# Experts' last biases gathered per slot, and rows gathered by a table of token ids, in a two-layer attention and mixture-of-experts kernel

## The chip, the cores and the metric

The kernel runs on one core of a Trainium2 chip. The metric is the device time of one execution in microseconds (us). Engines are called as in the profile: PE is the matmul engine and PEld its weight load, DVE the vector engine, ACT the scalar engine, POOL the GpSimd engine; SP issues most DMA transfers. POOL issues the indirect ones, whose rows are chosen by a list of indices in on-chip memory. On-chip memory has 128 partitions; sums of matmuls are made in PSUM banks[...].

## The reference

All arrays are fp32. There are 8 sequences of 256 tokens, 2048 tokens of 512 channels. Layer 0 adds a linear attention with decay and a mixture of experts to its input; layer 1 adds a small attention and a low-rank feed-forward part with gates. What the change touches is the mixture of experts of layer 0, cut to what matters:

```python
scores = softmax(xt @ router_w + router_b) + router_bias
g = scores.reshape(T, 4, 4)                   # 16 experts in 4 groups
keep the 2 groups with the largest maximum; of them the 2 best experts per token
gate[token, expert] = scores where chosen, else 0
for w1, b1, w2, b2, w3, b3, ge in experts:    # 512 -> 128 -> 512
    h = silu(xt @ w1 + b1) * (xt @ w2 + b2)
    y = y + ge[:, None] * (h @ w3 + b3)
z = silu(xt @ sw1 + sb1) * (xt @ sw2 + sb2) @ sw3 + sb3   # shared expert, all tokens
x = x + attention(xn) + y + z
```

The third biases are thus 16 rows b3 of 512 numbers, each added with the token's gate, and one row sb3 that every token gets once. The kernel's input `b3` holds them as 17 rows, the shared one last.

## The kernel before, in words

**Tiling.** Tokens are handled in 4 chunks of 512 (NCH = 4, `i` counts them), each of 4 tiles of 128 tokens (TPC = 4, `t` counts them; 16 tiles in all, NTT).

**The opening (to about 200 us).** The loop over chunks at lines 423–442 does, per chunk: transposes of the normalized rows on PE (`turn_rows`, L243), the store of the rows to DRAM (`xnd`), token differences on POOL (`token_sums`), the shared expert's first matmuls (`shared_up`, projected at L312), and `route` (matmuls at L271, then a chain on DVE: scores, `first_two` over groups, `first_two` over experts, the gates `ge`). Then `decays(i)`, `clear(i)`, and `share(i - 1)` for the chunk before. `share` calls `shared_down`, L329–341: it turns the gates with a column of ones (17 columns) by four transposes L333, ACT copies them to `geT` (L335), and for every tile a matmul L338 multiplies the turned gates with the 17 rows of b3 (two PE instructions each) ahead of the shared expert's own last matmul L340 into the same bank. So y's bias term and sb3 enter x here. DVE adds the bank to x, and x goes to DRAM as `xr`. `clear(i)` writes zeros over a fourth of `xd`, a DRAM array of 6016 slots of 512 numbers, 47 tiles of 128 slots.

**The dispatch.** Lines 447–523, mostly on DVE, give each token's two choices a slot so that every tile of 128 slots belongs to one expert: `slots` (token to slots), `slot_gates` (the two gates), `rows_` (which rows of the packed expert weights a tile needs). `before`, a table for ties, `sel_all` (the choices) and the gates live in the pool `work1` of the opening, which is given back by `opening.close()` at L525; the attention part's pool gets the same memory, so its first writes there wait for the dispatch.

**The long part (to about 2560 us).** A plan of units (chunk, group of heads) with seven products each (p1 to p7; Strassen's scheme, `product`, L666) runs inside a schedule in which ACT and POOL keep the written order, and PE, DVE and SP are ordered by a scheduler. `slot()`, L679, is called after each product: a slot takes about 1.39 us, 49 of them make a unit. In each slot up to one or two pieces of other work are written in, from a list to which `later(after, f)` adds `f`, due `after` slots on; pieces named in a tuple in `slot` don't count against that limit. Chunk 0 is computed with plain products while the weights' sums for the later chunks are made. In it, `row` loads each tile of normalized rows from `xnd` and `scatter` (L1094) writes it twice, by `slots`, into `xd` with indirect DMAs.

From the eighth unit on (chunk 1), `expert(j)` is written in for each of the 47 tiles, three per unit in seven units, two per unit after that. `Expert.__init__` takes a staging buffer `xw` (two exist, shared with other staging), loads the tile's rows from `xd` by SP (L696) and gathers the expert's weights by POOL (L697); `turn` (+8 slots) transposes the rows on PE (L706), `up` (+11) makes 8 matmuls (L716), silu on ACT, the product `he` on DVE; `down` (+14) multiplies by the third weight (L728), ACT copies the bank to `ye` (L733), SP stores it to `yd`.

At a chunk's end, `load_sum` (L933) loads `xr` into a staging buffer, and `done` (L939) makes the norm's root mean squares and `finish` (L586) adds the attention's sum to it on DVE; the result is stored as `xs_`. For the last chunk `next_x(3)` (L1289) loads `xr` and finishes it inside layer 1. `gather` and `settle` later fetch from `yd` each token's two rows and add them with `slot_gates`.

Of the kernel before, what the change touches and what calls it, by code (L numbers as in the profile page):

```python
# [66 lines left out]
def block_kernel(  # L67
# [75 lines left out]
    def once(shape, name):  # L143
        return work.tile(shape, FP, tag=name, name=name, bufs=1)

    scratch = big("scratch").rearrange("p (h b) n -> p h (b n)", h=4)
# [18 lines left out]
    b3_t = held[0 : E + 1, SH * C : (SH + 1) * C]  # L165
    nc.sync.dma_start(out=b3_t, in_=b3)
# [8 lines left out]
    xd = dram.tile([NSLOT, C], FP, name="xd")  # L175
# [7 lines left out]
    xnd = [dram.tile([P, TPC, C], FP, name=f"xnd{i}") for i in range(NCH)]  # L183
# [5 lines left out]
    zero = held[:, (SH + 1) * C : (SH + 2) * C].unsqueeze(1)  # L189
    nc.gpsimd.memset(zero, 0.0)  # L190
# [10 lines left out]
    before = once([P, E, E], "before")  # L201
# [8 lines left out]
    dist = const.tile([P, S + P], FP, name="dist")  # L210
# [54 lines left out]
    def route(xT, ge, sel):  # L265
# [40 lines left out]
        tt(ge[:, :, 0:E], sc, sel, ALU.mult)  # L306
        nc.vector.memset(ge[:, :, E : E + 1], 1.0)
# [21 lines left out]
    def shared_down(i, hT):  # L329
        xc = xs[i]  # L330
        pg = ps_sc()
        for t in range(TPC):
            nc.tensor.transpose(pg[0 : E + 1, bass.ts(t, P)], gates[i][:, t, :], ident)  # L333
        gT = work.tile([E + 1, CH], FP, tag="geT", name="geT", bufs=1)
        nc.scalar.copy(gT, pg[0 : E + 1, :])  # L335
        for t in range(TPC):
            py = ps_mm()
            mm(py, gT[:, bass.ts(t, P)], b3_t, start=True, stop=False)  # L338
            for e in range(SH):
                mm(py, hT[:, e, bass.ts(t, P)], w3sh[:, e, :], start=False, stop=(e == SH - 1))  # L340
            tt(xc[:, t, :], py, xc[:, t, :], ALU.add)
# [3 lines left out]
    sel_all = once([P, NTT, E], "sel_all")  # L345

    def share(i, hT):
        shared_down(i, hT)
        nc.sync.dma_start(out=xr[i], in_=xs[i])
# [60 lines left out]
    def clear(i):  # L410
        lo, hi = (0, 12, 24, 36, NMT)[i : i + 2]
        nc.sync.dma_start(
            out=xd[lo * P : hi * P, :].rearrange("(j p) c -> p j c", p=P),
            in_=zero.to_broadcast([P, hi - lo, C]),
        )

# [6 lines left out]
    for i in range(NCH):  # L423
        xT.append(work.tile([P, NC, CH], FP, tag="xT", name=f"xT{i}", bufs=3))
        for t in range(TPC):
            turn_rows(xT[i], xns[i], t, ps_mm())
        nc.sync.dma_start(out=xnd[i], in_=xns[i])
        if i + 1 < NCH:
            begin(i + 1)
        token_sums(i)  # L430
        if i == 0:
            for p in ORDER[0:2]:
                w = big("w")
                nc.sync.dma_start(out=w[:, 0:4], in_=w_att[0, RAW[p]])
                first_w.append(w)
        ups.append(shared_up(i))
        ge = once([P, TPC, E + 1], f"ge{i}")
        route(xT[i], ge, sel_all[:, bass.ts(i, TPC), :])
        gates.append(ge)
        decays(i)  # L440
        clear(i)
        if i > 0:
            share(i - 1, ups[i - 1])
# [6 lines left out]
    disp = Parts(accp.tile([P, 7 * CH], FP, tag="acc", name="disp"))  # L450
# [50 lines left out]
    nc.vector.tensor_reduce(own, owner, AX.X, ALU.add)  # L501
    nc.vector.tensor_scalar(own, own, float(E - 1), float(P), ALU.min, ALU.mult)
# [14 lines left out]
    for n in range(TOP):  # L517
        tt(hit, slot, ends_[:, n, :].unsqueeze(2).to_broadcast(full), ALU.is_equal)
        tt(hit, hit, sel_all, ALU.mult)
        for i in range(NCH):  # L520
            at_i = bass.ts(i, TPC)
            tt(hit[:, at_i, :], hit[:, at_i, :], gates[i][:, :, 0:E], ALU.mult)
# [63 lines left out]
    def finish(i, r):  # L586

        for b in range(2):
            for t in range(2):
# [4 lines left out]
                )  # L594

# [3 lines left out]
    with tc.tile_pool(name="attn", bufs=1) as attn, tc.manual_schedule(engines={mybir.EngineType.Activation, mybir.EngineType.Pool}):  # L599
# [79 lines left out]
        def slot():  # L679
# [3 lines left out]
            while pieces and pieces[0][0] <= now[0] and n < (2 if len(pieces) > 12 else 1):  # L683
                f = pieces.pop(0)[2]
                f()
                n += getattr(f, "func", f).__name__ not in ("silu", "gate", "row", "scatter", "load_sum", "sums1", "sums2", "sums3", "sums4", "settle0", "settle1", "out_sum")


        class Expert:


            def __init__(self, j):
# [3 lines left out]
                nc.sync.dma_start(out=self.xe, in_=xd[bass.ts(j, P), :])  # L696
# [6 lines left out]
            def turn(self):  # L703
# [4 lines left out]
                nc.vector.tensor_copy(self.xeT, pt.rearrange("p (c n) -> p c n", c=NC))  # L708

# [16 lines left out]
            def down(self):  # L726
# [6 lines left out]
                nc.scalar.copy(ye, py)  # L733
# [76 lines left out]
        class Unit:  # L810
# [122 lines left out]
            def load_sum(self):  # L933

                if self.i + 1 < NCH:
                    self.r = spare8()
                    nc.sync.dma_start(out=self.r, in_=xr[self.i])

# [141 lines left out]
        def expert(j):  # L1080
            e = Expert(j)
            later(8, e.turn)
            later(11, e.up)
            later(14, e.down)

        def row(t):

            x_ = attn.tile([P, C], FP, tag="sum", name="row", bufs=3)
            nc.sync.dma_start(out=x_, in_=xnd[t // TPC][:, t % TPC, :])
            for n in range(TOP):  # L1090
                later(6 + 10 * n, partial(scatter, x_, t, n))

        def scatter(x_, t, n):
            nc.gpsimd.indirect_dma_start(  # L1094
                out=xd[:, :],
                out_offset=bass.IndirectOffsetOnAxis(ap=slots[:, n, t : t + 1], axis=0),
                in_=x_, in_offset=None, bounds_check=NSLOT - 1, oob_is_err=False,
            )
# [78 lines left out]
        for n, (i, g, p) in enumerate(plan):  # L1177
# [6 lines left out]
            if k == 0:  # L1184
# [5 lines left out]
                if i == 0:  # L1190
                    for e in range(2):
                        later(1 + 24 * e, partial(row, 2 * g + e))
# [96 lines left out]
    def next_x(i):  # L1289
# [4 lines left out]
        else:  # L1294
            nc.sync.dma_start(out=x_, in_=xr[i])
            finish(i, x_)
# [325 lines left out]
```

## Time and profile before

| what | value |
|---|---|
| median of 3 runs | 2861.57 us (2854.19 to 2862.28) |
| the profiled execution, its own time | 2856.16 us |
| its span, first to last instruction | 2854.4 us |
| mean granted PE clock | 0.993 |
| transferred | 763.21 MB, of which 53.79 MB by POOL's queue |
| turns of the gates, L333 | 16 instructions, 272 ns each |
| bias matmuls, L338 | 32 instructions, 640 to 763 ns each by bank |
| ACT's copies of `ye`, L733 | 47, 585 ns each, 27.5 us |
| weight gathers on POOL, L697 | 47, 1.01 us each |
| row scatters on POOL, L1094 | 32, 1.08 us each |
| gathers of results on POOL, L556 | 32, 1.05 us each |
| POOL's sums of 128 x 512 | 1.27 us each |
| DVE's sums of 128 x 512 from PSUM | 0.69 us each |
| stores of zeros | 3 of 3072 KB, 1 of 2816 KB |

The profile is that of one execution, so its durations belong to 2856.16 us. Busy times of the engines overlap. A line of the form `PE ps_b L666 <- ACT c L1010` says that PE's instructions of line 666, with output in `ps_b`, waited for ACT's instruction of line 1010 that wrote `c`. L97 is the helper through which most elementwise operations go, so its instructions are told apart by tile names. An indirect DMA on POOL shows the time of its issue; when its data land is given apart.

### The profile page before, as it was taken

To read this page: it belongs to the slowest core of one execution; us is meant where nothing else is said; L and a number is where in the kernel's file an instruction comes from. 1 tells how busy PE (TensorE), PEld (TensorE's weight loads), DVE (VectorE), ACT (ScalarE), POOL (GpSimd) and SP (SyncE) were. 2 spreads that over 40 slices of the span, in tenths; PEclk is the share of its full clock that TensorE was granted. 3 is DMA by queue.
4 is the path that set the end of the run, shared out by engine and by line. 5 is a ranking of instruction groups with operands and counts; after the bars stand their busy time and mean duration, and the time that the engine had idled before them with its cause. 6 is when DMAs were issued, how large, how long until landed. Compare 5 with 4: busy or idle time off the path is not lost. (4 is left out here: it accounts for less than half of the span.)

```text
span 2854.4 us, 49572 instructions
## 1 busy us (share of the span) xinstructions
PE 2796.7 (98%) x19864; PEld 2566.1 (90%) x19864; DVE 1569.7 (55%) x2615; ACT 948.2 (33%) x1683; POOL 1465.7 (51%) x1213
## 2 busy tenths in 40 slices
PE   8989999999999999999999999999999999999999
PEld 4469999999999999999999999999999999987877
DVE  6555666666654445444545555555555555556663
ACT  3312222212244333333443333443444333432221
POOL 4545666665546555555645454545544566552210
PEclk9999999999999999999999999999999999999999
DMA  7888998899986777778877777777777788652211
GB/s 255 301 309 337 357 352 341 341 349 347 364 320 246 262 266 273 282 270 299 296 265 257 264 266 265 259 274 280 284 259 259 267 310 298 222 212 88 76 61 61
DMA packets 161943, 763.21 MB, mean 267 GB/s; under 512 B 18209, under 2 KB 24225, under 8 KB 109874
## 3 DMA queue, kind: packets, MB, share of 16 engines
q1 hardware_dynamic: 149826, 706.25, 66.9%
q0 software_dynamic: 11888, 53.79, 5.2%
q8 instruction: 157, 2.57, 0.4%
q14 instruction: 72, 0.59, 0.1%
HBM read 596.14 MB, written 163.05 MB: 266 GB/s over the span
## 5 line engine op out<-in xcount | busy, mean ns | idle before, releaser
L666 PE MATMUL ps_a<-xt,w 128*128 128x128 f32 x5376 | 750.9, 276 | 11.7 <-DVE r L97 7.7
L666 PEld LDWEIGHTS ps_a<-xt,w 128*128 128x128 f32 x5376 | 681.9, 192 | 30.1 <-issue 14.3
L97 POOL TENSOR_TENSOR c<-c 128x512 f32<-128x512 f32 x216 | 271.7, 1273 | 262.0 <-DVE c L97 259.9
L97 POOL TENSOR_TENSOR c<-c,r 128x512 f32<-128x512 f32 x240 | 318.4, 1347 | 158.9 <-DVE r L97 153.1
L666 PE MATMUL ps_e<-xt,w 128*128 128x128 f32 x2688 | 373.4, 275 | 1.3 <-DVE c L97 1.3
L97 POOL TENSOR_TENSOR sums<-sums,sq 128x512 f32<-128x512 f32 x120 | 153.3, 1278 | 426.4 <-ACT sq L796 425.6
L996 ACT COPY cp<-ps_a 128x512 f32<-128x512 f32 x336 | 196.4, 585 | 476.0 <-PE ps_a L666 468.8
L666 PEld LDWEIGHTS ps_e<-xt,w 128*128 128x128 f32 x2688 | 344.4, 192 | 11.2 <-issue 3.8
L97 POOL TENSOR_TENSOR w<-w 128x512 f32<-128x512 f32 x224 | 294.6, 1325 | 108.2 <-issue 31.2
L666 PE MATMUL ps_a<-w,xt 128*128 128x128 f32 x1792 | 346.7, 275 | 0.0
L858 PE MATMUL ps_sc<-wo,gT 128*128 128x256 f32 x1288 | 305.1, 379 | 1.8 <-POOL gT L97 1.8
L97 DVE TENSOR_TENSOR acc<-ps_sc,acc 128x512 f32<-128x512 f32 x208 | 143.3, 690 | 265.8 <-PE ps_sc L858 198.8
L666 PEld LDWEIGHTS ps_a<-w,xt 128*128 128x128 f32 x1792 | 272.3, 192 | 0.0
L97 DVE TENSOR_TENSOR c<-ps_a,c 128x512 f32<-128x512 f32 x232 | 157.9, 686 | 202.7 <-PE ps_a L666 201.7
L858 PEld LDWEIGHTS ps_sc<-wo,gT 128*128 128x128 f32 x1288 | 232.3, 190 | 26.8 <-POOL gT L97 2.0
L666 PE MATMUL ps_b<-xt,w 128*128 128x128 f32 x1680 | 236.4, 277 | 6.8 <-ACT c L1010 4.2
L801 DVE SCALAR_TENSOR_TENSOR gT<-ps_o,nw,c 128x256 f32<-128x256 f32 x256 | 112.0, 479 | 231.0 <-ACT sq L796 222.0
L666 PEld LDWEIGHTS ps_b<-xt,w 128*128 128x128 f32 x1680 | 217.3, 194 | 17.5 <-issue 8.2
L744 ACT ACTIVATE c<-c 128x512 f32<-128x512 f32 x256 | 148.9, 627 | 170.1 <-DVE c L97 170.0
L796 ACT ACTIVATE sq<-ps_o 128x512 f32<-128x512 f32 x120 | 71.6, 597 | 382.3 <-PE ps_o L782 382.3
L666 PE MATMUL ps_e<-w,xt 128*128 128x128 f32 x896 | 173.2, 275 | 0.0
L97 DVE TENSOR_TENSOR s<-ps_sc,decay 128x384 f32<-128x384 f32 x256 | 139.8, 552 | 40.7 <-PE ps_sc L770 38.1
(299 smaller groups left out, 4635.8 us busy)
## 6 DMA issues: line engine op xcount, KB each, us to landing
w<-in_w_att_dram SPq DMA_DIRECT2D x128, 1024.0 KB
st<-in_w_att_dram SPq DMA_DIRECT2D x32, 1024.0 KB
wo<-in_w_out_dram SPq DMA_DIRECT2D x113, 256.0 KB
decay<-dec SPq DMA_DIRECT2D x64, 384.0 KB
w<-ws0p SPq DMA_DIRECT2D x12, 1792.0 KB
w<-ws1p SPq DMA_DIRECT2D x12, 1792.0 KB
w<-ws2p SPq DMA_DIRECT2D x12, 1792.0 KB
w<-ws3p SPq DMA_DIRECT2D x12, 1792.0 KB
```

What stands on the lines that cost most here:

```text
L97: (eng or nc.vector).tensor_tensor(o, a, b, op)
L666: mm(bank[:, bass.ts(ty, P)], a, b, start=(first and ty == 0), stop=True, skip_group_check=True,)
L744: nc.scalar.activation(qk, qk, AF.Silu)
L796: nc.scalar.activation(sq, po, AF.Square)
L801: nc.vector.scalar_tensor_tensor(gT[:, h, :].rearrange("p (t n) -> p t n", t=2), po[:, bass.ts(h, S)].rearrange("p (t n) -> p t n", t=2), ...
L858: mm(py[:, bass.ts(t, S)], self.O[p][:, hh, bass.ts(t, P)], self.wo[p][:, hh, :], start=(t == 0 and hh == 0), stop=(hh == 1), skip_group_c ...
L996: nc.scalar.copy(c, bank)
```

## The change

Rows are no longer scattered. A DRAM array `table` of 6016 token ids (4 bytes each), allocated last, is zeroed once; chunk 0's units scatter into it the ids of each tile of tokens, twice (32 indirect DMAs of 128 ids), five per unit. In the last unit of chunk 0, `read_table` loads it as 47 rows of 128 ids, and 16 slots later DVE converts them, PE transposes them once and DVE writes `whose`, the ids with a slot tile per column. An expert's rows are then gathered by POOL from `xnd`, which is now one array of 2048 rows. `xd`, its zeros and `row` are gone.

The gates have no column of ones, and `shared_down` neither turns them nor multiplies by b3. Instead, after `turn` has read an expert's rows, `bias` gathers into the same buffer, for each of the 128 slots, the b3 row of the tile's expert (`own_`, one row 128 times), and DVE adds the bank and this to make `ye`; the gates are applied by `settle` as before. The shared row is added in `last_bias`: SP loads it to all partitions, POOL adds it to four tiles, in `load_sum` for chunks 0 to 2 and in `next_x` for chunk 3. The pieces of an expert are due at +10, +12 (`bias`), +13 and +18. `before`, `sel_all` and the gates move from `work1` to `disp`, which lies in the memory of the accumulators; `dist` moves from the constants to `work1`; the store of `xr` keeps its place in the program's order.

```diff
...
-    def once(shape, name):
-        return work.tile(shape, FP, tag=name, name=name, bufs=1)
+    def once(shape, name, dtype=FP):
+        return work.tile(shape, dtype, tag=name, name=name, bufs=1)
+    disp = Parts(accp.tile([P, 7 * CH], FP, tag="acc", name="disp"))
     scratch = big("scratch").rearrange("p (h b) n -> p h (b n)", h=4)
...
     nc.sync.dma_start(out=bsh_t, in_=b_sh)
-    b3_t = held[0 : E + 1, SH * C : (SH + 1) * C]
-    nc.sync.dma_start(out=b3_t, in_=b3)
     for i in range(1, NCH):
...
     dram = ctx.enter_context(tc.tile_pool(name="dram", bufs=1, space=bass.MemoryType.DRAM))
-    xd = dram.tile([NSLOT, C], FP, name="xd")
     yd = dram.tile([NSLOT, C], FP, name="yd")
...
     ]
-    xnd = [dram.tile([P, TPC, C], FP, name=f"xnd{i}") for i in range(NCH)]
+    xnd = dram.tile([NT, C], FP, name="xnd")
     dec = [dram.tile([P, 2, S + P], FP, name=f"dec{n}") for n in range(H // 2)]
...
     xr = [dram.tile([P, TPC, C], FP, name=f"xr{i}") for i in range(NCH)]
-    zero = held[:, (SH + 1) * C : (SH + 2) * C].unsqueeze(1)
-    nc.gpsimd.memset(zero, 0.0)
+    table = dram.tile([NSLOT, 1], I32, name="table")
+    none = once([NMT, P], "none", I32)
+    nc.gpsimd.memset(none, 0)
+    nc.sync.dma_start(out=table.rearrange("(j p) o -> j (p o)", p=P), in_=none)
...
-    before = once([P, E, E], "before")
+    before = disp.tile([P, E, E], FP, name="before")
     nc.gpsimd.memset(before, 1.0)
...
-    dist = const.tile([P, S + P], FP, name="dist")
+    dist = once([P, S + P], "dist")
     nc.gpsimd.iota(
...
         first_two(sel, masked, E)
-        tt(ge[:, :, 0:E], sc, sel, ALU.mult)
-        nc.vector.memset(ge[:, :, E : E + 1], 1.0)
+        tt(ge, sc, sel, ALU.mult)
...
         xc = xs[i]
-        pg = ps_sc()
-        for t in range(TPC):
-            nc.tensor.transpose(pg[0 : E + 1, bass.ts(t, P)], gates[i][:, t, :], ident)
-        gT = work.tile([E + 1, CH], FP, tag="geT", name="geT", bufs=1)
-        nc.scalar.copy(gT, pg[0 : E + 1, :])
         for t in range(TPC):
             py = ps_mm()
-            mm(py, gT[:, bass.ts(t, P)], b3_t, start=True, stop=False)
             for e in range(SH):
-                mm(py, hT[:, e, bass.ts(t, P)], w3sh[:, e, :], start=False, stop=(e == SH - 1))
+                mm(py, hT[:, e, bass.ts(t, P)], w3sh[:, e, :], start=(e == 0), stop=(e == SH - 1))
             tt(xc[:, t, :], py, xc[:, t, :], ALU.add)
     xT, gates, xns = [], [], []
-    sel_all = once([P, NTT, E], "sel_all")
+    sel_all = disp.tile([P, NTT, E], FP, name="sel_all")
...
         shared_down(i, hT)
-        nc.sync.dma_start(out=xr[i], in_=xs[i])
+        tc.keep_in_program_order(nc.sync.dma_start(out=xr[i], in_=xs[i]))
...
-    def clear(i):
-        lo, hi = (0, 12, 24, 36, NMT)[i : i + 2]
-        nc.sync.dma_start(
-            out=xd[lo * P : hi * P, :].rearrange("(j p) c -> p j c", p=P),
-            in_=zero.to_broadcast([P, hi - lo, C]),
-        )
     def begin(i):
...
             turn_rows(xT[i], xns[i], t, ps_mm())
-        nc.sync.dma_start(out=xnd[i], in_=xns[i])
+        nc.sync.dma_start(
+            out=xnd[i * CH : (i + 1) * CH, :].rearrange("(t p) c -> p t c", p=P), in_=xns[i]
+        )
         if i + 1 < NCH:
...
         ups.append(shared_up(i))
-        ge = once([P, TPC, E + 1], f"ge{i}")
+        ge = disp.tile([P, TPC, E], FP, name=f"ge{i}")
         route(xT[i], ge, sel_all[:, bass.ts(i, TPC), :])
...
         decays(i)
-        clear(i)
         if i > 0:
...
     rows_ = const.tile([P, NMT], I32, name="rows_")
-    disp = Parts(accp.tile([P, 7 * CH], FP, tag="acc", name="disp"))
+    own_ = const.tile([P, NMT], I32, name="own_")
+    whose = const.tile([P, NMT], I32, name="whose")
+    token = const.tile([P, NTT], I32, name="token")
+    nc.gpsimd.iota(token, pattern=[[P, NTT]], base=0, channel_multiplier=1)
...
     nc.vector.tensor_reduce(own, owner, AX.X, ALU.add)
+    nc.vector.tensor_scalar(own_, own, float(E - 1), None, ALU.min)
     nc.vector.tensor_scalar(own, own, float(E - 1), float(P), ALU.min, ALU.mult)
...
             at_i = bass.ts(i, TPC)
-            tt(hit[:, at_i, :], hit[:, at_i, :], gates[i][:, :, 0:E], ALU.mult)
+            tt(hit[:, at_i, :], hit[:, at_i, :], gates[i], ALU.mult)
         nc.vector.tensor_reduce(slot_gates[:, n, :], hit, AX.X, ALU.add)
...
                 )
+    def last_bias(r, t3):
+        nc.sync.dma_start(out=t3, in_=b3[E : E + 1].to_broadcast([P, C]))
+        for t in range(TPC):
+            add(r[:, t, :], r[:, t, :], t3, nc.gpsimd)
...
                 f()
-                n += getattr(f, "func", f).__name__ not in ("silu", "gate", "row", "scatter", "load_sum", "sums1", "sums2", "sums3", "sums4", "settle0", "settle1", "out_sum")
+                n += getattr(f, "func", f).__name__ not in ("silu", "bias", "gate", "read_table", "scatter", "load_sum", "sums1", "sums2", "sums3", "sums4", "settle0", "settle1", "out_sum")
...
                 self.xe, self.we = xw[:, 0:C], xw[:, C:]
-                nc.sync.dma_start(out=self.xe, in_=xd[bass.ts(j, P), :])
+                nc.gpsimd.indirect_dma_start(
+                    out=self.xe, out_offset=None, in_=xnd[:, :],
+                    in_offset=bass.IndirectOffsetOnAxis(ap=whose[:, j : j + 1], axis=0),
+                    bounds_check=NT - 1, oob_is_err=False,
+                )
                 nc.gpsimd.indirect_dma_start(
...
                 nc.vector.tensor_copy(self.xeT, pt.rearrange("p (c n) -> p c n", c=NC))
+            def bias(self):
+                nc.gpsimd.indirect_dma_start(
+                    out=self.xe, out_offset=None, in_=b3[:, :],
+                    in_offset=bass.IndirectOffsetOnAxis(ap=own_[:, self.j : self.j + 1], axis=0),
+                    bounds_check=E, oob_is_err=False,
+                )
...
                 ye = attn.tile([P, C], FP, tag="sum", name="ye", bufs=3)
-                nc.scalar.copy(ye, py)
+                add(ye, py, self.xe)
                 nc.sync.dma_start(out=yd[bass.ts(self.j, P), :], in_=ye)
...
                     nc.sync.dma_start(out=self.r, in_=xr[self.i])
+                    last_bias(self.r, attn.tile([P, C], FP, tag="sum", name="sb3", bufs=3))
...
             e = Expert(j)
-            later(8, e.turn)
-            later(11, e.up)
-            later(14, e.down)
-        def row(t):
-            x_ = attn.tile([P, C], FP, tag="sum", name="row", bufs=3)
-            nc.sync.dma_start(out=x_, in_=xnd[t // TPC][:, t % TPC, :])
-            for n in range(TOP):
-                later(6 + 10 * n, partial(scatter, x_, t, n))
-        def scatter(x_, t, n):
+            later(10, e.turn)
+            later(12, e.bias)
+            later(13, e.up)
+            later(18, e.down)
+        def scatter(t, n):
             nc.gpsimd.indirect_dma_start(
-                out=xd[:, :],
+                out=table[:, :],
                 out_offset=bass.IndirectOffsetOnAxis(ap=slots[:, n, t : t + 1], axis=0),
-                in_=x_, in_offset=None, bounds_check=NSLOT - 1, oob_is_err=False,
+                in_=token[:, t : t + 1], in_offset=None, bounds_check=NSLOT - 1, oob_is_err=False,
             )
+        def read_table():
+            rows = attn.tile([P, P], I32, tag="h1", name="rows")
+            nc.sync.dma_start(out=rows[0:NMT], in_=table.rearrange("(j p) o -> j (p o)", p=P))
+            byno = attn.tile([P, P], FP, tag="he", name="byno")
+            def turn_table():
+                nc.vector.tensor_copy(byno[0:NMT], rows[0:NMT])
+                pt = ps_sc()
+                nc.tensor.transpose(pt[:, 0:NMT], byno[0:NMT, :], ident[0:NMT, 0:NMT])
+                nc.vector.tensor_copy(whose, pt[:, 0:NMT])
+            later(16, turn_table)
...
                 if i == 0:
-                    for e in range(2):
-                        later(1 + 24 * e, partial(row, 2 * g + e))
+                    for e in range(5 * g, min(5 * g + 5, TOP * NTT)):
+                        later(5 + 10 * (e - 5 * g), partial(scatter, e // TOP, e % TOP))
+                    if g == NG - 1:
+                        later(4, read_table)
                 if i == NCH - 1 and g in (NG - 4, NG - 3):
...
             nc.sync.dma_start(out=x_, in_=xr[i])
+            last_bias(x_, work.tile([P, C], FP, tag="sb3", name="sb3", bufs=1))
             finish(i, x_)
```

## The prediction

> **What bounds the kernel now.** I read the page's busy shares first, then a table of windows that cuts the span by stage, then what TensorE (PE) waited for, then the timeline of the opening.
>
> Page, part 1 (busy us, share of the span, instructions):
> ```profile
> PE 2796.7 (98%) x19864; PEld 2566.1 (90%) x19864; DVE 1569.7 (55%) x2615; ACT 948.2 (33%) x1683; POOL 1465.7 (51%) x1213
> ```
> PE is the bound: time goes only where PE work goes, or where a PE gap opens or closes. Windows (stretch, its length, busy us of PE, PEld, DVE, ACT, POOL, PE clock, DMA share, GB/s):
> ```profile
> 60.00:164.00 104.00, 95.09 (x272) 43.24 (x273) 54.95 (x111) 30.25 (x48) 53.96 (x84) 0.93 0.78 291
> 164.00:200.00 36.00, 27.79 (x217) 26.67 (x217) 24.02 (x55) 6.84 (x11) 7.24 (x6) 0.95 0.84 310
> 200.00:764.00 564.00, 559.34 (x4328) 539.82 (x4327) 348.84 (x537) 122.34 (x211) 345.08 (x271) 1.00 0.91 346
> 764.00:2430.00 1666.00, 1655.78 (x12633) 1576.64 (x12632) 849.27 (x1286) 660.46 (x1183) 903.02 (x705) 1.00 0.76 276
> ```
> The opening (60–200) has 17 us without PE work in 140, at a clock of 0.93–0.95; the two long stages have 15 in 2230 at full clock. What can be won lies in the opening; what can be lost, in the rest. PE's waits, 130–210 us, then 764–2430:
> ```profile
> PE ps_b L666 <- ACT c L1010: 4.2, 1, 4.2
> PE ps_sc L333 <- DVE ge L97: 3.6, 1, 3.6
> PE ps_a L666 <- issue: 2.2, 1, 2.2
> ...
> PE ps_a L666 <- DVE r L97: 6.0, 16, 0.4
> PE ps_sc L858 <- POOL gT L97: 1.8, 1, 1.8
> PE ps_e L666 <- DVE c L97: 1.3, 2, 0.6
> ```
> PE in the opening (start, us, operation, wait):
> ```profile
> 97.62 0.60 PE L333 MATMUL ps_sc<-ident,ge 128*17 128x128 f32 x4
> 98.88 1.12 PE L338 MATMUL ps_b<-held,geT 17*128 17x512 f32 x2 [0.66 <-ACT geT L335]
> 99.93 1.98 PE L340 MATMUL ps_b<-held,scratch 128*128 128x512 f32 x4
> ...
> 147.41 0.61 PE L333 MATMUL ps_sc<-ident,ge 128*17 128x128 f32 x4 [3.58 <-DVE ge L97]
> ...
> 175.97 1.55 PE L666 MATMUL ps_b<-xt,w 128*128 128x128 f32 x6 [4.20 <-ACT c L1010]
> ```
> Each chunk pays for turned gates and bias matmuls; the last turn waits for the router; after the first products PE waits 4.2 us for an ACT copy into memory that the opening's dispatch tensors still hold. DVE's router chain of the last chunk, which ended on PE at 130.65 (DVE's timeline, same columns):
> ```profile
> 130.83 0.23 DVE L97 TENSOR_TENSOR sc<-ps_sc,rb 128x64 f32<-128x64 f32 x1 [0.87 <-PE ps_sc L271]
> ...
> 145.73 1.07 DVE L263 TENSOR_SCALAR sel_all<-sel_all 128x64 f32<-128x64 f32 x1
> 146.83 0.53 DVE L97 TENSOR_TENSOR ge<-sc,sel_all 128x64 f32<-128x64 f32 x1
> ```
> Some 16 us from the router's sums to `ge`: that chain stays.
>
> **What the Trainium skill says.** "Perfetto Trace Analysis", Optimization Strategy: gaps are to be sought on the bound engine within each regime; I do. Same page, DMA Instruction — SWDGE (GPSIMD): the profiled instruction ends when its descriptors are made, not when data land. The trace agrees: the weight gather L697 takes 1.01 us on POOL and lands after 6.9/7.5/13.0 us (min/median/max). "DMA: Bandwidth & Descriptors", Issuing engines are not separate DMA queues: transfers of all engines share 16 DMA engines, so bytes removed count anywhere. "TensorE: Matmul & The Clock Gate", What's actually happening: an idle window of about 3.4 us drops the clock to half. The trace agrees: after the 3.6 us wait the clock falls, and L338 takes about 2.07 us for two instead of 1.12.
>
> **The change, part by part.** *Opening, PE.* Per chunk the turns and their copy go: 60.60 − 59.34 = 1.26 us, ×4 = 5.0. L338 costs about 1.05 a pair (98.88 to 99.93), that is 1.05 × 16 = 16.8. The wait on `ge` (3.6) goes, and the slow-clock stretch after it (149–156, 2–3 us). That is 27–28 us if nothing else takes over. But the next chunk's x transposes, and the dispatch, wait for DVE, whose chain ends about 15 us after route's last matmul. So I place each step by whichever of PE and that chain is later. Chunk 1 to 2: shared_up starts at about 74.3 instead of 80.3, −6.0. Chunk 2 to 3: 14.6 after route instead of 17.7, −3.0, DVE-bound. Chunk 3 to the first product: 15.3 after route's end (130.65) instead of 33.7, less 1.9 of dispatch matmuls that now stand among the products, −16.5. (PE then has nothing that waits for `ge`; the turns, bias pairs and slow clock that stood in these 33.7 are gone together.) Then product p6, the first that reads weight differences which DVE makes after the dispatch chain: 36.9 after route's end instead of 56.1. PE would be there 9 us earlier than DVE and other work fills part: about 5.5 us of new stall at p6 against the 4.2 us stall that goes because `sel_all`, `before` and the gates leave the memory that ACT's copies reuse. By p6 −28.2 in all with the steps above (6.0 + 3.0 + 16.5 + 2.7 of clock); the 2.2 us "issue" stall near 199 mostly goes: **−29.5** by 210 us. If the chain bound every step, 20; if PE did, 33.
>
> *Chunk 0 (210–764).* Gone: clears 12.3 MB, row loads 4.2, row scatters 8.4, together 24.9 MB; the DMA share was 0.91 there, but PE waited only 4.7 us for anything. Scatters of 128 × 4 bytes replace those of 256 KB at the same ~1.08 us on POOL. The table's load and one transpose (two DVE copies, one PE matmul) cost 0.5 (in the sum below) and must precede the gathers; they have 16 slots of 1.39 us between them. SP's queue is also rid of 16 row loads and four clears of 3 MB, ahead of which no weight load can pass. **−1.5** (bounds 0 and the 4.7).
>
> *Experts (764–2430).* Per tile: one SP load becomes a POOL gather, plus a bias gather: 94 × 1.01 = 95 us, POOL 903 to 998 of 1666 (60%). ACT loses 47 × 0.585 = 27 us, DVE gains 47 × 0.69 = 32 (849 to 881): both have room. POOL was busy without a break at 826–844 and 1289–1304 and PE lost 1.5 us in the whole of 764–1308, so POOL's lateness is covered by several us: +1. The bias goes into the buffer that the turn has read, one slot ahead of `up`, and must be there when `down` ends: by the written slots 17 tiles have 8.6 us, 13 have 10–12, 17 have 12–14. Nearest row, 128 rows of 2 KB: L556, 3.8/6.2/8.9 us to landing; L697, the weights:
> ```profile
> DMA to landing us min/median/max: 6.9/7.5/13.0
> ```
>  Price below: 2.0 us fixed + 256 KB at 436 GB/s, about 2.6 (the skill's "DMA: Bandwidth & Descriptors", Anatomy of one DMA — SWDGE (gpsimd) path; no row here is that short); above: 13.0, the longest L697. I take 7.5, plus the wait for POOL's turn. DVE's add then waits now and then; behind it stand DVE's sums `c` for the next product, PE has products ahead: +2. Only two `xw` buffers exist, and now the second tile's sits until its add; expert 1's turn comes 3.1 us of PE work later than expert 0's down while gather (7.5) and issue (0.9) must pass: PE stalls once, **+4**.
>
> *Shared bias.* Three times in load_sum (chunks 0–2): 4 POOL adds × 1.27 = 5.1 us behind two loads; queued behind them are POOL's sums for products; at 774.96 POOL sat idle 9.9 us before such sums, so mostly covered: +4 in all. Once in next_x(3): DVE's finish waited 1.9 us for the load (2728.3) and PE 1.85 for DVE after it; 5.1 us of POOL now stand between. PE's next product waits that much less what covers it: **+3**. Table +0.5.
>
> Sum: −29.5 − 1.5 + 1 + 2 + 4 + 4 + 3 + 0.5 = **−16.5**. The profiled execution took 2856.2 us (span 2854.4): 2839.7. The median of the runs stands 5.4 above it, 2845.1 from there; three runs spread over 8. I take **2843**.
>
> **Rivals.** *B, later costs hidden.* The landing is nearer 6 us, POOL keeps up, chunk 0 gains 3: only +4 to +5 remains, −28: 2832. For: PE lost just 15 us in 2230. Against: the third bias and `xw` buffer are real orders in time. *C, given back.* DVE adds wait 2 us on the 30 early tiles and half of it reaches PE (+30 × 0.5 = 15 over forecast), or the router's chain lets only 20 of the 29.5 through (+9.5): 2853–2859. For: DVE's chain is 15 us at each chunk. *D, slower: the bias gather lands late.* All 128 rows of one gather read the same 2 KB of `b3`, which no row of the profile shows; if that takes 13 us, 17 tiles wait 4.4 us and 13 wait 2.3 on DVE, 105 us; PE's lead absorbs about 2 per tile, 45 us stay: 2843 + 45 = 2888. It decides from about 25–30 us of added PE waiting, a landing of 11 to 12 us. Against: gathers of the same size land in at most 8.9. *E, the opening gets nothing:* the bound there is DVE and DMA, and PE's lost work turns into waiting. Against: PE waited only 5.3 us on DVE there (3.6 for `ge`, 1.7 for `w`) while 22 us of its own work goes; time would be 2861 + 14.5 = 2876 at worst; inside D's chance.
>
> **How the numbers follow.** A change under 0.3% (8.6 us) can't be told from none. Forecast 0.50 (own range 2835–2852), B 0.22, C 0.16 (mostly within 0.3%, a part beyond it on the faster side), D 0.12. Range: from B's lower end (2825: all later costs nil, −31, and the median's noise) to where C ends and D begins, 2866. Leaving out most of D and some of B's tail, 2 in 10. Faster: 0.50 + 0.22 + a little of C, less noise, 0.74; same 0.13; slower 0.13.
>
> **What would show it.** PE's part of 60–200 should lose about 20 us of work, L333 and L338 should be gone, the first L666 should start near 146 instead of 164, with a new wait on DVE `w` near p6. In 764–2430 PE's busy time stays 1655 and waits grow from about 10 to 17–20, with one L706 wait of about 4 on a gather at expert 1. The new add of `ye` should wait for DMA under 2 us on the mean; above 4 is D. DVE's finish in next_x(3) should stand behind four POOL adds, some 5 us after the load lands where it was 0. Wrong would be: PE idle in 200–764 growing (transfers now colliding earlier), a POOL backlog that delays sums, or a slower landing of the 2 KB row gathers of `xnd`.

## The result, and the profile after

The changed kernel takes 2977.14 us (median of 4 runs, 2974.82 to 2982.32) against 2861.58 us before: 1.0412 times as long, 95% interval 1.039 to 1.0435. That is 116 us slower where some 19 us faster were forecast, and outside the range. The profiled execution took 2975.54 us, its span is 2973.8 us.

The page of the changed kernel, busy shares, and two rows of the 40 slices of its span:
```profile
PE 2808.0 (94%) x19817; PEld 2587.0 (87%) x19817; DVE 1600.8 (54%) x2661; ACT 920.9 (31%) x1631; POOL 1576.5 (53%) x1324
...
PE   7978888878999999999999999999999999999999
...
DMA  6799988987888777777787777778777778653211
```
PE has 47 instructions fewer, the bias matmuls among those gone, and yet more busy time (2808.0 against 2796.7 us, at a mean clock of 0.976 against 0.993). It is short of work in the first ten slices only, to about 740 us. The windows by stage (length, busy us of PE, PEld, DVE, ACT, POOL, clock, DMA share, GB/s):
```profile
60.00:150.00 90.00, 80.67 (x271) 45.72 (x270) 54.59 (x118) 21.54 (x35) 48.52 (x81) 0.87 0.70 264
...
200.00:764.00 564.00, 469.46 (x3405) 447.17 (x3404) 265.56 (x426) 98.58 (x170) 274.98 (x220) 0.92 0.90 261
764.00:2430.00 1666.00, 1643.79 (x12539) 1565.02 (x12538) 886.54 (x1333) 613.95 (x1095) 991.50 (x795) 1.00 0.77 280
```
Chunk 0 (200–764) is where the time went: 95 us of it without PE work instead of 5. The DMA engines are as busy as before (0.90 against 0.91), but they move 261 GB/s instead of 346. Busy engines that move a quarter less are the sign that transfers take longer, not that there are more. PE's waits there:
```profile
PE ps_sc L888 <- DVE gT L811: 52.6, 9, 10.5
PE ps_sc L779 <- DVE acc L97: 24.4, 3, 9.2
PE ps_b L664 <- DMA w<-in_w_att_dram: 7.9, 2, 5.5
```
DVE's own queue was behind: its waits between 200 and 740 us begin with these two, sums of attention weights that wait for loads of 1 MB:
```profile
DVE w L97 <- DMA w<-in_w_att_dram: 125.5, 14, 19.7
DVE w L97 <- DMA st<-in_w_att_dram: 35.3, 5, 15.1
```
In the kernel before, the two were:
```profile
DVE w L97 <- DMA st<-in_w_att_dram: 11.8, 4, 4.1
...
DVE w L97 <- DMA w<-in_w_att_dram: 9.6, 3, 3.5
```
What lengthens the loads shows in narrow windows of the changed kernel. POOL issued a scatter of token ids at 221.52 us (same columns):
```profile
220.00:222.00 2.00, 2.00 (x18) 1.95 (x18) 0.85 (x2) 0.00 (x0) 1.77 (x3) 1.00 0.98 407
222.00:224.00 2.00, 2.00 (x18) 1.95 (x18) 0.00 (x0) 0.54 (x1) 1.98 (x3) 1.00 0.75 307
224.00:226.00 2.00, 2.00 (x18) 1.95 (x18) 1.91 (x4) 0.05 (x1) 1.05 (x1) 1.00 0.83 57
226.00:228.00 2.00, 2.00 (x18) 1.95 (x18) 0.58 (x2) 1.12 (x2) 0.00 (x0) 1.00 0.59 78
228.00:230.00 2.00, 2.00 (x16) 1.90 (x15) 0.01 (x1) 0.00 (x0) 0.00 (x0) 1.00 1.07 184
230.00:232.00 2.00, 2.00 (x15) 1.87 (x14) 0.00 (x0) 1.04 (x3) 0.00 (x0) 1.00 0.61 156
232.00:234.00 2.00, 2.00 (x14) 1.82 (x13) 0.00 (x0) 0.97 (x3) 0.42 (x1) 1.00 0.99 418
```
For 8 us after a transfer of 512 bytes in all, everything together moves 57 to 184 GB/s, on the mean 119, where it moved some 415; then it is back. That is 8 × (1 − 119/415) = 5.7 us of all DMA engines for this one scatter. Over all 32 it is less: in the 14 us from the start of each (or up to the next one) the engines were busy 4.5 us longer, on the mean, than the bytes moved then would take at the rate of the rest of the stage (383 GB/s at full share), 143 us in sum. Chunk 0 had some slack in its transfers and lost 120 us. The ids' landing, 8.3/10.1/11.7 us (min/median/max), is longer than that of the 256 KB scatters that they replace (6.7/7.3/8.2, in the kernel before).

To follow the loss, I take the instructions of ACT that write `c` from `c`, in order of time, in both traces, and compare the starts of each with its counterpart. The changed kernel is 21.0 us ahead at the first, 1.5 ahead at 318 us, 99 behind at 866 us, 115 behind at 1625 us, 116 behind at 2650 us; the spans differ by 119.

### The profile page after: what moved, and what is told of

It is laid out like the page before. It is cut to its first block, busy times and chain, and to the rows that moved or that the text cites. A ratio compares the mean times of both kernels' runs of the same rounds, so it can differ in the third digit from the quotient of the medians.

```text
span 2973.8 us, 49621 instructions
## 1 busy us (share of the span) xinstructions
PE 2808.0 (94%) x19817; PEld 2587.0 (87%) x19817; DVE 1600.8 (54%) x2661; ACT 920.9 (31%) x1631; POOL 1576.5 (53%) x1324
## 4 chain that ended last, share of the span: by engine, by line
PE 75%; DMA 12%; DVE 7%; issue 3%; POOL 2%; ACT 1%; SPq 0%; DVEq 0%; POOLq 0%; ACTq 0%
PE ps_a L664 21%; PE ps_e L664 11%; PE ps_sc L868 9%; DMA w<-in_w_att_dram 7%; PE ps_b L664 6%; PE ps_o L791 3%; PE ps_sc L779 3%; PE ps_sc L888 3%; PE ps_sc L726 3%; PE ps_a L1535 2%; PE ps_o L792 2%; PE ps_sc L780 2%; DVE w L97 1%; DVE r L97 1%; PE ps_sc L738 1%
## 5 line engine op out<-in xcount | busy, mean ns | idle before, releaser
L868 PE MATMUL ps_sc<-wo,gT 128*128 128x256 f32 x1288 | 304.8, 379 | 1.8 <-POOL gT L97 1.8
L888 PE MATMUL ps_sc<-wo,gT 128*128 128x256 f32 x576 | 148.3, 404 | 52.8 <-DVE gT L811 52.8
L97 DVE TENSOR_TENSOR w<-w,st 128x512 f32<-128x512 f32 x128 | 89.5, 736 | 185.1 <-DMA w<-in_w_att_dram 141.1
```

The lines of the kernel that those rows point to most:

```text
L97: (eng or nc.vector).tensor_tensor(o, a, b, op)
L868: mm(py[:, bass.ts(t, S)], self.O[p][:, hh, bass.ts(t, P)], self.wo[p][:, hh, :], start=(t == 0 and hh == 0), stop=(hh == 1), skip_group_c ...
L888: mm(py[:, bass.ts(h, S)], gT[:, hh, bass.ts(t, P)], self.wo[pair, h][:, hh, :], start=(h == 0 and hh == 0), stop=(hh == 1), skip_group_ch ...
```

## The experiments

The kernel before was timed again beside each group of experiments, with medians of 2857.20 to 2858.52 us; the ratios below are to these.

**Theory A:** scatters of 4-byte ids hold up all transfers; A1, because a write of 4 bytes is slow in itself; A2, because ids of one expert, whose slots are neighbours, are written side by side. **Theory B:** without the 12.3 MB array the others moved in DRAM, and loads beside stores in chunk 0 became slow. What speaks for B is only that the stage with both loads and large stores is the one that got slower.

**Ids in rows of 512 bytes.**
```diff
-    table = dram.tile([NSLOT, 1], I32, name="table")
+    table = dram.tile([NSLOT, P], I32, name="table")
...
-                in_=token[:, t : t + 1], in_offset=None, ...
+                in_=token[:, t : t + P], in_offset=None, ...
...
-            nc.sync.dma_start(out=rows[0:NMT], in_=table.rearrange("(j p) o -> j (p o)", p=P))
+            nc.sync.dma_start(
+                out=rows[0:NMT].unsqueeze(2), in_=table.rearrange("(j p) o -> j p o", p=P)[:, :, 0:1]
+            )
```


> The changed kernel, with only the table widened: each slot has a row of 512 bytes, and a scatter writes the whole row (the id and 508 bytes of no use), so that no write is of 4 bytes. Theory A (each scatter of 4-byte ids holds up all DMA engines for some 5 us, and chunk 0's weights come late for that): the loss of some 120 us between 190 and 700 us goes; about 2860, within 15. Theory B (the removal of the 12.3 MB array moved the arrays in DRAM and slowed loads beside stores in chunk 0): nothing changes, about 2975.

Measured: 2894.94 us, 1.0124 (1.0091 to 1.0156) of the kernel before. The loss in chunk 0 is gone up to 680 us (PE is 15 to 31 us ahead of the kernel before), but then some 35 us are lost at one place. DVE's waits, 680–760 us:
```profile
DVE byno L1117 <- DMA rows<-table: 30.6, 1, 30.6
```
This is the experiment's own cost: the table is read as 6016 pieces of 4 bytes, and DVE's first instruction that needs it holds up all others behind it; PE waits 29.1 us behind DVE. SP was held as well: the issue of its four loads right behind the read took 38.75 us, and 2.6 us in the kernel with rows of 188 bytes below:
```profile
679.86 38.75 SPq L925 DMA_DIRECT2D wo<-in_w_out_dram  x4
```
So the value missed A's 2860 by the read, which I had not priced.

**4 bytes into the same rows of 512 bytes.** The index is the slot times 128, into a table of single ids; the row's rest is not written.
```diff
+    nc.vector.tensor_scalar(far_, ends_, float(P), None, ALU.mult)
...
-                out_offset=bass.IndirectOffsetOnAxis(ap=slots[:, n, t : t + 1], axis=0),
+                out_offset=bass.IndirectOffsetOnAxis(ap=far_[:, n, t : t + 1], axis=0),
```


> The changed kernel with the same wide table, but each scatter writes only the 4 bytes of the id into its own row of 512 bytes. Theory A1 (4-byte writes are slow in themselves): as slow as the changed kernel, about 2970. Theory A2 (they are slow because ids of one expert share the same 512 bytes, so that engines write into one line by turns): fast as with wide rows, about 2860. Theory B (arrays moved in DRAM): about 2975, with packets slow at all times and not after scatters alone.

Measured: 2896.22 us, the same as with whole rows, with the same 29.1 us of PE's waiting behind the read. Each scatter is again 128 writes of 4 bytes, issued at 223.66 us here, and the others don't notice it:
```profile
222.00:224.00 2.00, 2.00 (x18) 1.95 (x17) 0.00 (x0) 1.83 (x4) 1.84 (x3) 1.00 1.01 426
224.00:226.00 2.00, 2.00 (x18) 1.95 (x18) 0.13 (x1) 1.60 (x3) 0.74 (x2) 1.00 1.04 430
226.00:228.00 2.00, 2.00 (x18) 1.95 (x18) 1.90 (x4) 0.59 (x1) 1.18 (x1) 1.00 0.98 406
228.00:230.00 2.00, 2.00 (x18) 1.95 (x18) 1.43 (x3) 0.00 (x0) 0.00 (x0) 1.00 1.03 426
```
After 230 us the rate falls here too, but with it the share of busy engines (0.53, then 0.08): there was little left to move. So A1 falls: 4 bytes alone cost nothing here.

**No scatters.**
```diff
-    nc.gpsimd.memset(none, 0)
+    nc.gpsimd.iota(none, pattern=[[16, P]], base=0, channel_multiplier=0)
...
-                        later(5 + 10 * (e - 5 * g), partial(scatter, e // TOP, e % TOP))
+                        pass
```


> The changed kernel without the 32 scatters of ids; the table is filled at the start with multiples of 16, so the experts gather rows spread over the tokens, but not their own: the dispatch of rows is left out of the computation. Theory A: the stall of chunk 0 goes, about 2850 to 2860. Theory B: about 2975.

Measured: 2845.8 us, 0.9959 (0.9948 to 0.9969). With the scatters alone away and every array where the changed kernel has it, the kernel is 11.5 us below the kernel before at the median: theory B can't hold. (The traced execution, 2854.09 us, is the slowest of its 18.)

**The kernel before, with the scatters added.** The source is the slot numbers themselves, so nothing else is needed.
```diff
+        def ids(t, n):
+            nc.gpsimd.indirect_dma_start(
+                out=table[:, :],
+                out_offset=bass.IndirectOffsetOnAxis(ap=slots[:, n, t : t + 1], axis=0),
+                in_=slots[:, n, t : t + 1], in_offset=None, bounds_check=NSLOT - 1, oob_is_err=False,
+            )
```


> The kernel before, with 32 scatters of 4-byte numbers added at the slots of chunk 0 where the changed kernel has them, into a table allocated last that nothing reads. All other arrays stay where they were. Theory A: chunk 0 loses what it lost in the changed kernel, about 2960 to 3000. Theory B: 32 more issues of 1 us on POOL, about 2862 to 2870.

Measured: 2981.61 us, 1.0439 (1.0402 to 1.0476): 124 us for 32 transfers of 512 bytes; besides them only a table and its zeros were added. It is 130 us behind at the end of chunk 0 and 130 at the end. Its chunk 0, in which the DMA engines are never free and move 272 GB/s instead of 346:
```profile
200.00:764.00 564.00, 477.90 (x3429) 455.68 (x3429) 257.75 (x423) 96.58 (x167) 295.62 (x243) 0.92 0.99 272
```
The ids' landing in it:
```profile
DMA to landing us min/median/max: 9.2/11.9/15.3
```

**The table turned.** Slot r of tile j is written to row r, place j, so ids of neighbouring slots of one tile lie a row apart: 512 bytes in the first kernel, 188 bytes in the second, whose table has as many bytes as the changed kernel's. The table is read straight into `whose`, with no transpose.
```diff
+    nc.vector.tensor_scalar(tile_of, ends_, -63.5, 1.0 / P, ALU.add, ALU.mult)
+    nc.vector.tensor_scalar(tile_of, tile_of, 12582912.0, None, ALU.add)
+    nc.vector.tensor_scalar(tile_of, tile_of, -12582912.0, float(1 - 47 * P), ALU.add, ALU.mult)
+    nc.vector.scalar_tensor_tensor(places, ends_, float(47), tile_of, ALU.mult, ALU.add)
...
+            nc.sync.dma_start(out=whose, in_=table.rearrange("(p j) o -> p (j o)", p=P)[:, 0:NMT])
```
(12582912 is 1.5 × 2^23: added and taken off, it rounds to a whole tile number.)

> The changed kernel with the table turned: slot r of tile j goes to row r of 128 rows, place j, rows 512 bytes apart (64 KB in all). Ids of one expert, which have neighbouring slots, then lie 512 bytes apart; each scatter still writes 128 times 4 bytes, and the table is read as 128 rows straight into the index tile, with no transpose. Theory A2 (writes into one and the same 512 bytes hold each other up): no stall in chunk 0, and no slow read as in the wide table: about 2846, like the kernel without scatters. Theory A1 (a 4-byte write is slow by itself): about 2970.

> The same turned table without gaps: rows 188 bytes apart, 24 KB in all, as large as the changed kernel's; only the order of the ids in it differs. If writes must share 512 bytes to hold each other up: some are left (two to three rows of 188 bytes in 512), a part of the loss stays, 2860 to 2920. If only much nearer neighbours do (64 bytes or less), it goes: about 2846.

Measured: 2856.94 us, 0.9988 (0.9975 to 1.0002), and 2851.07 us, 0.9981 (0.9965 to 0.9997). The first is with rows of 512 bytes, the second with 188. The order of 6016 ids in 24 KB was worth 126 us. By their ratios to the kernel before, both are 6 to 8 us above the kernel without scatters. The interval of the second overlaps with that kernel's, so its 6 us are not certain.

**Ids 64 bytes apart.** As with the wide table, the slot times 16.
```diff
+    nc.vector.tensor_scalar(far_, ends_, 16.0, None, ALU.mult)
```


> The changed kernel with slots' ids 64 bytes apart (neighbouring slots of one expert in neighbouring 64 bytes), 4-byte writes. Up to the read of the table at 690 us: if writes hold each other up within 512 bytes, chunk 0 loses as in the changed kernel, over 100 us by then; if only within 64 bytes, nothing is lost and PE is some 15 to 20 us ahead of the kernel before at 660 us. After it the slow read of 6016 elements costs some 30 us, as it did with the wide table. So about 2980 or more, or about 2895.

Measured: 2895.34 us: nothing lost up to 680 us (15.8 us ahead), then the slow read, as in the wide table. While it runs, hardly anything else moves; the window of that wait:
```profile
686.00:716.00 30.00, 4.02 (x35) 3.77 (x33) 0.00 (x0) 0.00 (x0) 1.02 (x1) 0.65 0.10 1
```
So the writes hold up the transfers when they are side by side, and not at 64 bytes. Where between 4 and 64 bytes it begins was not tried.

The reckoning over all scatters (with the result, above; the same 383 GB/s) says the same. With ids side by side the engines are busy 4.5 us too long for each in the changed kernel, and 5.4 us in the kernel before with scatters added. With ids 64 or 512 bytes apart, and in both turned tables, it is 0.2 us, about as much as with whole rows of 512 bytes or of 2 KB.

How long the rows of neighbours are depends on the routing, and no trace shows the places. Worked out from the reference with its own inputs (seed 0), the routing is lopsided: two of the 16 experts get 2048 and 1859 of the 4096 choices. Then the 128 ids of a scatter form only one to four solid pieces, some 512 bytes in all; in the turned tables, about 5 of the 127 pairs of neighbours in a scatter are nearer than 64 bytes. Whether the short pieces of an even routing, some 8 ids each, would cost as much is not shown.

**The table first in DRAM.** The turned table of 24064 bytes before all other arrays.
```diff
+    table = dram.tile([P * 47, 1], I32, name="table")
     yd = dram.tile([NSLOT, C], FP, name="yd")
```


> The turned table without gaps allocated as the first array in DRAM, so that all other arrays of the kernel begin 24064 bytes later and none keeps to a multiple of 128 KB. If where the arrays begin matters, loads and stores of 1 to 1.8 MB take longer, 2 per cent or more in chunk 0, where the DMA share is highest; if not, about 2851, as with the table last.

Measured: 2857.65 us (2850.07 to 2866.39), 0.9993 (0.9982 to 1.0004), against 2851.07 (2847.81 to 2864.54) with the table last. Chunk 0 is not 2 per cent (11 us) longer: from 200 to some 760 us the kernel loses 14 us of its lead, as with the table last. The intervals of the two ratios overlap (0.9965 to 0.9997 with the table last), so whether some microseconds hang on the place stays open.

**The experts' pieces.** In the changed kernel PE's waits from 764 to 2550 us begin with these:
```profile
PE ps_sc L726 <- DVE xeT L710: 7.7, 6, 1.3
PE ps_a L664 <- DVE r L97: 7.4, 15, 1.7
PE ps_e L664 <- DVE c L97: 5.9, 2, 4.2
PE ps_sc L868 <- POOL gT L97: 1.8, 1, 1.8
PE ps_sc L708 <- DMA xw<-xnd,whose: 1.3, 1, 1.3
```
The first is `up` too near to `turn`. I wrote up and down later:
```diff
-            later(13, e.up)
-            later(18, e.down)
+            later(15, e.up)
+            later(20, e.down)
```


> The turned table with gaps, and an expert's up and down written two slots later (15 and 20 instead of 13 and 18). In the changed kernel PE waited 6 times 1.3 us before up for the copy of the turned rows. Theory: those 7.7 us go, 8 less than with the turned table alone, about 2838. Rival: the staging buffer is held longer and the third expert's gather comes late, so that nothing is won or some is lost.

Measured: 2855.77 us, 0.9985 (0.9971 to 0.9999), nothing won against the turned table alone. The six waits are gone, and one of the same sum stands at expert 1's turn (PE's waits, 780–1400 us):
```profile
PE ps_sc L714 <- DMA xw<-xnd,whose: 8.5, 1, 8.5
```
It is the rival: of two staging buffers, expert 0 holds one until its late `down`.

**The shared bias in the opening.**
```diff
         normalize(xns[i], xs[i])
+        for t in range(TPC):
+            add(xs[i][:, t, :], xs[i][:, t, :], sb3, nc.gpsimd)
```


> As the one before, and the shared bias is added by POOL to x in the opening, after x is normalized, instead of at the chunks' ends. Theory: POOL's sums at the chunk's ends and in layer 1 cost 3.4 and some 2 us of PE's waiting: 5 less, about 2833. Rival: POOL's 16 sums (20 us) in the opening delay token differences or the shared down sum, and the opening loses as much.

Measured: 2858.21 us, 0.9998 (0.9986 to 1.001). The wait at the first chunk's end fell from 3.9 to 1.7 us and that in layer 1 went (3.6), but at the first of the ACT instructions compared it was 15.8 us ahead of the kernel before, where the run before was 24.8 ahead. It looks like the rival again, but its size is uncertain: the turned table with gaps, which has the same opening as the run before, was 21.2 ahead.

**Earlier down, later sums.** Delays 9, 11, 13, 17, and the sums of the shared bias 11 slots behind their loads:
```diff
+                    later(11, self.add_last)
```


> The turned table without gaps; an expert's pieces at 9, 11, 13 and 17 slots, so that up stands further from turn without holding the staging buffer longer; and POOL's sums of the shared bias at the chunks' ends 11 slots after their loads instead of behind them at once. Theory: the waits before up (7.7 us) and part of the wait at the first chunk's end (3.4 us) go and none comes at expert 1's turn (8.5 us where up and down were two slots later): about 2843, 8 to 10 below the turned table alone. Rival: the time is set by DMA and DVE in chunk 0 and by the chunks' ends, not by these waits: 2850 to 2856.

Measured: 2856.3 us, 0.9988 (0.9974 to 1.0003). The experts' waits are gone without the one at expert 1, and the kernel is 22.7 us ahead at 1380 us, where the turned table was some 11 ahead. The later sums then gave it back at two chunks' ends (PE's waits, 764–2100 us):
```profile
PE ps_e L670 <- DVE c L97: 13.2, 2, 6.6
```

**The experts' delays alone.** The turned table (188 bytes), and:
```diff
-            later(10, e.turn)
-            later(12, e.bias)
+            later(9, e.turn)
+            later(11, e.bias)
             later(13, e.up)
-            later(18, e.down)
+            later(17, e.down)
```

> The turned table without gaps and the experts' pieces at 9, 11, 13 and 17 slots, with the shared bias added right behind its loads as in the changed kernel. In the run before, these delays took away all of PE's waits before up, and the later sums cost 6.6 us at each of two chunks' ends. Theory: without those, some 9 us less than that run: about 2847, and below the kernel before by some 10. Rival: the gain of the delays is lost at the first chunk's end whatever stands there: 2853 to 2857.

Measured: 2847.76 us (18 runs), 0.996 (0.9949 to 0.997) of the kernel before: about 10 us faster than it and 129 faster than the changed kernel. At the first chunk's end there is one wait of 4.4 us. Against the run before, which differs only in the place of the sums, it is some 8 us faster. What the delays alone add to the turned table isn't clear: 0.996 against 0.9981, with intervals that overlap. This is the version to keep: the change, with the table turned and the experts' pieces at 9, 11, 13 and 17.

## Why the prediction was wrong

**The step that failed** is in the part on chunk 0: "Scatters of 128 × 4 bytes replace those of 256 KB at the same ~1.08 us on POOL." I priced the issue, 1.00 us as measured, and counted the bytes. The price lay in how long the transfer held up the DMA engines: 4.5 us of all of them on the mean, 143 us in sum, and chunk 0 lost 120 us; added to the kernel before, the scatters cost 124 us. For the bias gather, which no row of the trace showed, the prediction gave a price below and one above; for a scatter of single words, side by side, it gave neither. I looked for the danger of many accesses to one place in the bias gather (rival D), where 128 reads of one row land well, and not in the ids, where 128 writes go to few places. The prediction's own first sign of being wrong did come, PE idle in 200–764 growing, from 5 to 95 us; the reason it gave, transfers colliding earlier, can account for no more than the 12 us without PE work that are left when the scatters go.

The bytes were misread as well. The zeros' 12.3 MB belong to the opening and not to chunk 0: their four stores were issued from 24.5 us on, the last as the line shows, and from 165 to 185 us no packet of their size (2048 bytes) ran.
```profile
145.92 0.43 SPq L412 DMA_DIRECT2D xd<-held  x1
```
So chunk 0 was rid of 12.6 MB, half of the 24.9.

**Rival D** named another place. The bias gather of the changed kernel landed after 4.2/5.4/7.5 us, and DVE's add waited for it in 6 of the 47 tiles, 10.9 us in sum (who waited for line 714):
```profile
  DVE ye L97: 10.9, 6
```

**The opening** came out in its sum, in part by luck, for its steps came otherwise. The first product starts near 146 by the forecast, at 143.96 in the trace, 20.4 us before its counterpart. But the last route ends at 130.29, only 0.5 us earlier than before, where the first two steps were to bring 9.0 (the 146 doesn't count these 9.0, the sum of 29.5 does); the way from there took 13.7 us instead of 33.6, 19.9 less where the third step had 16.5. PE then waited 0.7 us for the ACT copy instead of 4.2, and 4.6 for DVE `w`. That looks like the forecast stall at p6 (5.5), but without the hold-up by the ids the wait is 2.1 us at most and in the kernel without scatters isn't there; in the kernel before it was 1.7. The first product, and the one behind the ACT copy:
```profile
143.96 0.83 PE L664 MATMUL ps_b<-xt,w 128*128 128x128 f32 x6
...
153.22 0.94 PE L664 MATMUL ps_b<-xt,w 128*128 128x128 f32 x6 [0.68 <-ACT c L1021]
```
With the scatters away, the lead at some 200 us was 28.7 us (forecast 29.5).

**Chunk 0 without the hold-up** was mis-sized too: forecast −1.5, but the lead fell from 31.7 at 287 us to 19.7 at 747 us in the kernel without scatters, where PE's gaps sum to 11.6 us (4.7 before), which explains 7 of these 12. DVE there waited 85 us for loads of weights:
```profile
DVE w L97 <- DMA w<-in_w_att_dram: 85.2, 18, 9.7
```
In the kernel before, the same wait is 9.6 us. PE that starts 30 us earlier meets loads that don't come earlier by as much. This is read from the trace, not tested.

**The rest.** Forecast 11 us from experts and chunk ends, measured 15 to 17, by other items than mine. The one stall at expert 1's turn was 1.3 to 1.7 us, not 4; it is 8.5 where `down` is later, so the mechanism was right and the cover was better. Not foreseen were the 7.7 us before `up`. The chunks' ends cost about what was said: 4.2 at the first, where 0.6 was. In next_x(3) 3 us were forecast; spans and leads differ by 3.7 there. DVE's finish begins behind four POOL sums, PE waits behind DVE:
```profile
2844.23 5.74 DVE L584 SCALAR_TENSOR_TENSOR x<-acc,rms,x 128x512 f32<-128x512 f32 x4 [1.12 <-POOL x L97]
...
2842.93 5.83 POOL L97 TENSOR_TENSOR x<-x,sb 128x512 f32<-128x512 f32 x4 [19.01 <-DMA x<-xr]
...
2851.24 1.35 PE L1457 MATMUL ps_e<-t,fa 128*128 128x256 f32 x3 [3.54 <-DVE cp L97]
```
Without the ids' hold-up the number would have come close, 2843 against 2845.8 with no scatters, but partly by luck. The gain was 11.5 us, not 18.5: the kernel before had its median at 2857.27 in 23 runs beside it, where 2861.57 was known. And the parts of the traced execution give less still: 28.7 won in the opening, 9 lost up to 747 us where 1.5 were to be won, 15 lost by experts and chunk ends where 11 were forecast, and 2.5 in layer 1 leave 2 us.

## What to carry to other kernels

A transfer is priced by what it does to the others on the same engines, not by its bytes or by the issue alone: look at GB/s beside the DMA share in windows of a few microseconds around it. Lay out a table for scatters so that neighbours in the index are not neighbours in memory, and so that it is read in whole rows; here turning it cost four small instructions of DVE. When a stall is mended by moving a piece later, ask which buffer it then holds longer.

## What the runs showed that I had not expected

128 writes of 4 bytes side by side slow all transfers of the core for some 8 us: in the scatter shown to 57 to 184 GB/s from some 415, over all 32 by 4.5 us of all engines each. At 64, 188 or 512 bytes apart they leave no such mark (0.2 us each; 406 to 430 GB/s during the one shown). A read of 6016 single words, 64 or 512 bytes apart, was done some 39 us after its issue (678.6 to 717.8 us with 64 bytes); for 30 of these the core's DMA engines moved 1 GB/s at a share of 0.10, and the issue of SP's next four loads took 38.7. Whether the read held the other transfers or only kept them from being issued is not settled. The Trainium skill, "DMA: Bandwidth & Descriptors", Specifications, says that below 512 bytes the engines read, modify and write; these runs show that this alone is no price worth counting for 128 words (2896.22 us with words of 4 bytes, 2894.94 with whole rows of 512), and that the words' neighbourhood is. Why neighbours hold each other up, and why for all transfers, no run here shows.
